# Mamba with attention on one core: engines issuing in program order, and a norm factor left in PSUM

## The chip, the cores and the metric

The kernel runs on one core of a Trainium2 chip. The metric is device time in microseconds (us), of one launch. The core has a tensor engine (TensorE, PE in the profile), a vector engine (VectorE, DVE), a scalar engine (ScalarE, ACT), GpSimd (POOL) and a queue for transfers (SyncE, SP). Each engine works through its own stream of instructions, and semaphores hold an instruction back until what it needs is there. TensorE writes its results to PSUM; the other data lies in SBUF.

The kernel is written with a layer that takes instructions in the order of the source and puts them into an order of its own for each engine, by a model of when each will be ready. Which instruction stands before which is thus decided when the program is built, not while it runs.

## The reference

A stack of four Mamba layers on 8 images of 256 channels and 32 x 32 positions, then a squeeze-and-excitation gate with batch normalization, then three attention layers. Only the Mamba part is touched:

```python
def _mamba(xs, lw, lb, iw, cw, cb, xw, dw, db, alog, dp, ow):
    mu = xs.mean(-1, keepdims=True)
    var = ((xs - mu) ** 2).mean(-1, keepdims=True)
    xn = (xs - mu) * jax.lax.rsqrt(var + 1e-05) * lw + lb
    xin, z = jnp.split(xn @ iw.T, 2, axis=-1)
    xc = ...                     # causal convolution over 4 positions, for each channel
    xin = jax.nn.silu(jnp.swapaxes(xc, 1, 2))
    proj = xin @ xw.T
    dt = jax.nn.softplus(proj[..., :DTR] @ dw.T + db)
    Bm = proj[..., DTR:DTR + DS]
    Cm = proj[..., DTR + DS:]
    A = -jnp.exp(alog)
    def step(h, t):
        dt_t, b_t, c_t, x_t = t
        h = h * jnp.exp(dt_t[..., None] * A) + (dt_t * x_t)[..., None] * b_t[:, None, :]
        return (h, jnp.einsum('bdn,bn->bd', h, c_t))
    ...                          # scan over the 1024 positions
    y = jnp.swapaxes(ys, 0, 1) + xin * dp
    return y * jax.nn.silu(z) @ ow.T
```

## The kernel before

The work is cut into 64 units: 4 layers, 8 samples, and 2 chunks of 512 positions each. A unit has 16 steps (2 halves `q` of the channels, 8 groups `g` of two state elements each), 1024 steps in all. In each step TensorE forms the drive `bx` of the recurrence, VectorE runs four scans, GpSimd multiplies the states by C, and TensorE sums them into `y` two steps later. Beside the steps of unit n run, cut into pieces by `yield`, the front part of unit n+2 (`inward`), the middle part of unit n+1 (`onward`) and the end of unit n-1 (`outward`). `AT` says in which of the 16 steps (slots 0 to 15) a piece comes.

The tile pools that matter: `wk1` has one buffer for each tag, `wk2` two; `ps_b` has two PSUM buffers for `bx`, `ps_m` two for everything tagged `mm`; `dap` has eight buffers for the decays `da` (two steps); `h` and `ct` have three.

```python
LAG, AHEAD = 2, 2
AT = ((inward, 2, (0, 1, 2, 3, 5, 6, 8, 9, 11, 12, 13, 14)), (onward, 1, (1, 3, 5, 7, 8, 9, 10, 11, 12)),
      (outward, -1, (3, 4, 6, 7, 9, 10, 11, 12, 13)))
DIAGONALS = (4, 5, 6, 10, 11, 12, 13, 14)
for i in range(len(steps) + LAG):
    n, at = divmod(i, per_unit)
    if i < len(steps):
        ahead(i + AHEAD)                    # transfer of ct; four Exp on ScalarE: da
        bxs = [forced(*steps[i], k) for k in range(2)]      # TensorE: bx
        for k in range(2):
            state(i, k, bxs[k])             # VectorE: four scans
        product(i)                          # ScalarE: hc (first chunk); GpSimd: h * ct
    if i >= LAG:
        ...                                 # TensorE: y += h of step i - LAG; VectorE: gate at the end of a half
    ...                                     # the pieces that AT names for this slot
    if at in DIAGONALS and n + 1 < len(units):
        diagonal(units[n + 1])              # GpSimd: dg, one of eight
```

The front part, with the norm (cut):

```python
pmu = ps_m.tile([P, T], F32, name=f"pmu{u}", tag="mm")          # slot 0
for k in range(CT):
    nc.tensor.matmul(pmu, lhsT=mean_w, rhs=x[:, k, :], start=(k == 0), stop=(k == CT - 1))
xn = wk1.tile([P, CT, T], F32, name=f"xn{u}", tag="xn")
nc.vector.tensor_tensor(xn, x, pmu.unsqueeze(1).to_broadcast([P, CT, T]), ALU.subtract)     # L126
sq = wk1.tile([P, CT, T], F32, name=f"sq{u}", tag="sq")
nc.scalar.activation(sq, xn, AF.Square)
yield
pvar = ps_m.tile([P, T], F32, name=f"pvar{u}", tag="mm")        # slot 1
for k in range(CT):
    nc.tensor.matmul(pvar, lhsT=mean_w, rhs=sq[:, k, :], start=(k == 0), stop=(k == CT - 1))
rstd = sq[:, 0, :]
nc.scalar.activation(rstd, pvar, AF.Ln, bias=eps)
nc.scalar.activation(rstd, rstd, AF.Exp, scale=-0.5)
nc.vector.tensor_tensor(xn, xn, rstd.unsqueeze(1).to_broadcast([P, CT, T]), ALU.mult)       # L136
yield
...     # slots 2 to 14: pin (TensorE) and its copy xr or sz (ScalarE), convolution pc (TensorE) and its copy xin
for q in range(DT // 2):
    nc.scalar.activation(s["xin"][q], s["xin"][q], AF.Silu)     # L183
nc.scalar.activation(sz, sz, AF.Silu)                           # L184
exp_ln_table()                                                  # L108, a table preload
```

The middle part (cut). `one` and `dtx` share a tag with one buffer, as do `ln` and `sq`:

```python
for q in range(DT // 2):                                        # slots 3 and 5, 7 and 8
    dt = wk3.tile([P, 2, T], F32, name=f"dt{u}_{q}", tag="dt")
    e = wk1.tile([P, 2, T], F32, name=f"e{u}_{q}", tag="e")
    for r in range(2):
        pd = ps_m.tile([P, T], F32, name=f"pd{u}_{i}", tag="mm")
        nc.tensor.matmul(pd, ...)
        nc.scalar.activation(e[:, r, :], pd, AF.Abs, bias=col(V_DB + i))        # L224
        nc.scalar.activation(dt[:, r, :], pd, AF.Relu, bias=col(V_DB + i))      # L225
    nc.scalar.activation(e, e, AF.Exp, scale=-1.0)              # L226
    yield
    one = wk1.tile([P, 2, T], F32, name=f"one{u}_{q}", tag="dtx")
    nc.scalar.activation(one, e, AF.Identity, bias=1.0)         # L229
    ln = wk1.tile([P, 2, T], F32, name=f"ln{u}_{q}", tag="sq")
    nc.scalar.activation(ln, one, AF.Ln)                        # L231
    nc.vector.scalar_tensor_tensor(e, one, 1.0, e, ALU.subtract, ALU.subtract)  # L233
    nc.vector.tensor_tensor(dt, dt, e, ALU.subtract)            # L234
    nc.vector.tensor_tensor(dt, dt, ln, ALU.add)                # L235
    yield
for q in range(DT // 2):                                        # slots 9 and 10, 11 and 12
    dtx = wk1.tile([P, 2, T], F32, name=f"dtx{u}_{q}", tag="dtx")
    for i in range(2):
        nc.gpsimd.tensor_tensor(tokens(dtx[:, i, :]), halves(s["dt"][q][:, i, :]), halves(xin[q][:, i, :]), ALU.mult)   # L241
    yield
    ...     # TensorE: pt, the transposes of dtx; ScalarE: their copy dtxT
    yield
```

The end part, `outward`: the output projection `po` in two pieces of two matmuls for each half of the channels, and L278, which adds it to the residual.

## Time and profile before

| | |
|---|---|
| time, median of 3 | 10693.12 us (10679.93 to 10694.59) |
| span of the profiled execution | 10677.8 us |
| Mamba phase, from the first scan to the end of the last | 93.60 to 8004.30 us |
| attention phase after it | 2673.5 us |
| granted TensorE clock over the span | 0.961 |
| table loads on ScalarE | 519, 1283 ns each |

The lines of a profile name an engine, a line of the kernel (L385), the operation, what it writes and reads (`h<-da,bx`), shape and count. A group's numbers are the time that the engine was busy with it, the mean duration of one in ns, and the idle time before it with what ended that. A timeline's numbers are the start and the duration in us; a bracket at the end is the idle time just before and what ended it. Matmuls are pipelined and their ends are modelled, so a busy TensorE isn't TensorE at its peak.

### The profile page before, as it was taken

What the parts mean: (1) busy time and instruction counts of PE and PEld (TensorE: products, weight loads), DVE (VectorE), ACT (ScalarE), POOL (GpSimd) and SP (SyncE); (2) the same over time, 40 slices, a digit from 0 to 9 for tenths busy, and PEclk for the clock granted to TensorE, in tenths of its full rate; (3) what the DMA queues carried; (4) which work ended last, traced back from release to release, by engine and by line L of the source; (5) the groups of instructions that cost most, each with busy time, mean ns of one, the idle gap of its engine ahead of it and who ended that gap; (6) DMA issues with size and microseconds to landing.
All of it is one profiled execution on the core that took longest, in us unless ns stands there. A gap on an engine that the chain in (4) does not pass through costs nothing. (4 is left out here: it accounts for less than half of the span.)

```text
span 10677.8 us, 237971 instructions
## 1 busy us (share of the span) xinstructions
PE 9676.4 (91%) x104946; PEld 4868.8 (46%) x104946; DVE 7570.7 (71%) x6419; ACT 6108.2 (57%) x8477; POOL 6709.4 (63%) x2563
## 2 busy tenths in 40 slices
PE   7999998999999989999998988888888999999998
PEld 3444444444444444444444444444443433444433
DVE  4878877777878877877887777777785455544554
ACT  5666666666666766666666666666652233333333
POOL 5777776677777767777776766666671344344346
PEclk9999999999999999999999999999999999999999
DMA  1222222222222222222222222222221000000000
GB/s 64 81 86 86 89 81 81 81 86 84 88 83 82 87 82 86 87 83 84 84 85 83 89 86 86 86 88 88 89 100 40 5 9 9 7 6 1 5 5 9
DMA packets 212557, 704.91 MB, mean 66 GB/s; under 512 B 32640, under 2 KB 33728, under 8 KB 210880
## 3 DMA queue, kind: packets, MB, share of 16 engines
q1 hardware_dynamic: 211520, 689.61, 19.4%
q8 instruction: 830, 13.60, 0.5%
q14 instruction: 207, 1.70, 0.1%
HBM read 637.09 MB, written 52.43 MB: 65 GB/s over the span
## 5 line engine op out<-in xcount | busy, mean ns | idle before, releaser
L392 POOL TENSOR_TENSOR h<-h,ct 128x2048 f32<-128x2048 f32 x1024 | 4683.9, 4581 | 2007.1 <-ACT hc L391 921.9
L335 ACT ACTIVATE da<-dt,A 128x512 f32<-128x512 f32 x4096 | 2847.4, 718 | 2298.7 <-DVE h L385 2283.8
L385 DVE TENSOR_TENSOR_SCAN h<-da,hc,bx 128x512 f32<-128x512 f32 x2048 | 2456.9, 1258 | 692.7 <-PE bx L325 579.9
L385 DVE TENSOR_TENSOR_SCAN h<-da,bx 128x512 f32<-128x512 f32 x2048 | 2332.0, 1198 | 722.9 <-PE bx L325 658.9
L325 PE MATMUL bx<-dg,dtxT 64*64 64x128 f32 x65536 | 2316.7, 281 | 306.1 <-DVE h L385 293.9
L325 PEld LDWEIGHTS bx<-dg,dtxT 64*64 64x64 f32 x65536 | 1950.1, 137 | 1131.0 <-issue 933.4
L349 PE MATMUL y<-h,twin 64*64 64x512 f32 x16384 | 2048.5, 599 | 72.2 <-POOL h L392 72.2
L571 ACT ACTIVATE fp<-fs 128x1024 f32<-128x1024 f32 x768 | 765.4, 1022 | 1435.7 <-PE fs L566 1408.0
L142 PE MATMUL pin<-xn,win 128*128 128x512 f32 x2048 | 1015.9, 619 | 9.8 <-DVE xn L136 5.8
L349 PEld LDWEIGHTS y<-h,twin 64*64 64x64 f32 x16384 | 718.0, 135 | 668.9 <-issue 511.4
L166 PE MATMUL pc<-xr,cd 64*64 64x512 f32 x4096 | 654.1, 695 | 207.8 <-DVE xo L278 207.8
L566 PE MATMUL fs<-fq,fk 32*128 32x512 f32 (+1 forms) x3072 | 723.4, 649 | 56.2 <-ACT fp L652 39.3
L588 DVE TENSOR_TENSOR fz<-fz,fp 128x1024 f32<-128x1024 f32 x384 | 531.3, 1384 | 331.0 <-ACT fp L571 327.0
L588 POOL TENSOR_TENSOR fz<-fz,fp 128x1024 f32<-128x1024 f32 x192 | 477.6, 2487 | 416.2 <-ACT fp L571 412.4
L142 PEld LDWEIGHTS pin<-xn,win 128*128 128x128 f32 x2048 | 349.0, 190 | 676.0 <-issue 405.6
L274 PE MATMUL po<-sz,wo 128*128 128x512 f32 x1024 | 561.7, 676 | 52.3 <-ACT dt L225 52.3
L582 PE MATMUL fo<-fp,fv 128*32 128x512 f32 (+1 forms) x3072 | 597.2, 615 | 0.0
L241 POOL TENSOR_TENSOR dtx<-dt,xin 128x512 f32<-128x512 f32 x256 | 432.8, 1716 | 224.8 <-ACT ln L231 222.2
L256 POOL TENSOR_TENSOR dg<-twin,bt 128x512 f32<-128x512 f32 x512 | 539.0, 1064 | 50.8 <-PE bx L325 37.9
L166 PEld LDWEIGHTS pc<-xr,cd 64*64 64x64 f32 x4096 | 230.4, 154 | 597.2 <-issue 274.5
L235 DVE TENSOR_TENSOR dt<-dt,ln 128x1024 f32<-128x1024 f32 x128 | 470.4, 3675 | 14.4 <-ACT da L335 0.9
L566 PEld LDWEIGHTS fs<-fq,fk 32*128 32x128 f32 (+1 forms) x3072 | 196.1, 185 | 469.4 <-issue 270.2
(391 smaller groups left out, 9160.8 us busy)
## 6 DMA issues: line engine op xcount, KB each, us to landing
ct<-cdr SPq DMA_DIRECT2D x1024, 512.0 KB, 3.7
spill<-xo SPq DMA_DIRECT2D x72, 512.0 KB, 5.3
x<-spill SPq DMA_DIRECT2D x48, 512.0 KB, 4.9
xo<-spill SPq DMA_DIRECT2D x48, 512.0 KB, 3.5
x<-in_x SPq DMA_DIRECT2D x16, 512.0 KB, 5.0
xo<-in_x SPq DMA_DIRECT2D x16, 512.0 KB, 3.7
res<-in_x SPq DMA_DIRECT2D x16, 512.0 KB, 4.2
fx<-spill SPq DMA_DIRECT2D x16, 512.0 KB, 6.4
```

Source lines behind the costliest of these rows:

```text
L142: nc.tensor.matmul(ps, lhsT=w["in"][:, k, e * P:(e + 1) * P], rhs=xn[:, k, :], start=(k == 0), stop=(k == CT - 1))
L166: nc.tensor.matmul(pcs[r][e * H:(e + 1) * H, :], lhsT=w["cd"][r * H:(r + 1) * H, j * K + k, :], rhs=xr[r * H:(r + 1) * H, e, k:k + T], sta ...
L274: nc.tensor.matmul(po, lhsT=w["out"][:, i, m * P:(m + 1) * P], rhs=s["sz"][:, i, :], start=(i == 0), stop=(i == DT - 1))
L325: nc.tensor.matmul(bx[r * H:(r + 1) * H, t:t + H, :], lhsT=s["dtxT"][q][h * H:(h + 1) * H, i, k, r * H:(r + 1) * H], rhs=s["dg"][g][h * H: ...
L335: nc.scalar.activation(da, s["dt"][q][:, i, :], AF.Exp, scale=s["w"]["A"][:, nn:nn + 1])
L349: nc.tensor.matmul(s["y"][r][i * H:(i + 1) * H, :], lhsT=twin[r * H:(r + 1) * H, :], rhs=h[r * H:(r + 1) * H, i, j, :], start=False, stop= ...
L385: nc.vector.tensor_tensor_scan(hs[i][:, k, j, :], das[i][2 * k + j], bx[:, :, j], init, ALU.mult, ALU.add)
L392: nc.gpsimd.tensor_tensor(h, h, cts.pop(i).unsqueeze(1).to_broadcast([P, 2, NG, T]), ALU.mult)
L566: nc.tensor.matmul(scs[h // 2][:, h % 2, :], lhsT=k[r:r + D, m, kt * P:(kt + 1) * P], rhs=q[r:r + D, m, half * T:(half + 1) * T], start=Tr ...
L571: nc.scalar.activation(p, scs[j], AF.Exp, scale=scale)
L582: nc.tensor.matmul(acc["o"][r:r + D, :], lhsT=v[:, kt, m * P + r:m * P + r + D], rhs=ps[h // 2][:, h % 2, :], start=(kt == 0), stop=(kt == ...
L588: add(acc["z"][j], acc["z"][j] if kt > 1 else probs[i - 1][j], ps[j], ALU.add)
```

## The change

It has three parts. All compute engines in the Mamba phase get a wrapper that pins each instruction behind the one that the source has before it on the same engine; the queue for transfers keeps the layer's freedom. The factor of the norm, Ln and Exp of the variance, is written back into `pvar` in PSUM and read from there by VectorE, so that it doesn't occupy `sq`, which `ln` needs as well. And the second residual tile of the last layer's end part, `sx`, takes a buffer of `x` in a pool of two instead of the single one of `dtx`, which in a fixed order would still be held by an earlier user. What it is for: the layer's order rests on a model of the durations; the source order is the author's own plan, which keeps functions of one table together and puts nothing in front of what was meant to come first.

```diff
--- before.py
+++ after.py
@@ -37,8 +37,28 @@
 G_SEB2, G_BNW, G_BNB, G_BQ1, G_BK1, G_BO1, G_BQ2, G_BK2, G_BQ3, G_BK3, G_BO3, G_N = range(0, 24, 2)
 
 
+class InOrder:
+
+
+    def __init__(self, tc, engine):
+        self.tc, self.engine = tc, engine
+
+    def __getattr__(self, name):
+        def call(*args, **kwargs):
+            return self.tc.keep_in_program_order(getattr(self.engine, name)(*args, **kwargs))
+
+        return call
+
+
+class Engines:
+    def __init__(self, tc):
+        nc = tc.nc
+        self.tensor, self.vector, self.scalar, self.gpsimd = (InOrder(tc, e) for e in (nc.tensor, nc.vector, nc.scalar, nc.gpsimd))
+        self.sync = nc.sync
+
+
 def mamba_phase(tc, ctx, a, spill, ident, gvec, stats):
-    nc = tc.nc
+    nc = Engines(tc)
     cst = ctx.enter_context(tc.tile_pool(name="m_cst", bufs=1))
     wp = ctx.enter_context(tc.tile_pool(name="m_w", bufs=1))
     wk1 = ctx.enter_context(tc.tile_pool(name="m_wk1", bufs=1))
@@ -105,7 +125,7 @@
         nc.sync.dma_start(w["out"], a["m_out"][l])
 
     def exp_ln_table():
-        tc.keep_in_program_order(nc.scalar.preload_act_table_set("natural_log_exp_and_others"))
+        nc.scalar.preload_act_table_set("natural_log_exp_and_others")
 
     def tokens(t):
 
@@ -130,10 +150,9 @@
         pvar = ps_m.tile([P, T], F32, name=f"pvar{u}", tag="mm")
         for k in range(CT):
             nc.tensor.matmul(pvar, lhsT=mean_w, rhs=sq[:, k, :], start=(k == 0), stop=(k == CT - 1))
-        rstd = sq[:, 0, :]
-        nc.scalar.activation(rstd, pvar, AF.Ln, bias=eps)
-        nc.scalar.activation(rstd, rstd, AF.Exp, scale=-0.5)
-        nc.vector.tensor_tensor(xn, xn, rstd.unsqueeze(1).to_broadcast([P, CT, T]), ALU.mult)
+        nc.scalar.activation(pvar, pvar, AF.Ln, bias=eps)
+        nc.scalar.activation(pvar, pvar, AF.Exp, scale=-0.5)
+        nc.vector.tensor_tensor(xn, xn, pvar.unsqueeze(1).to_broadcast([P, CT, T]), ALU.mult)
         yield
 
         def in_proj(e):
@@ -304,7 +323,7 @@
         exp_ln_table()
         yield
         for h in range(NCH):
-            y = x if h == c else wk1.tile([P, CT, T], F32, name=f"sx{b}_{h}", tag="dtx")
+            y = x if h == c else wk2.tile([P, CT, T], F32, name=f"sx{b}_{h}", tag="x")
             if h != c:
                 nc.sync.dma_start(y, spill[b][h])
             r = wk1.tile([P, CT, T], F32, name=f"res{b}_{h}", tag="e")
```

## The prediction

> **What bounds the kernel now.** I read the page's first part for the engines, then the table of stretches for where the time lies, then the groups of instructions, then the timeline of one unit, because in a loop of waits the averages say little.

> The page's busy times (engine, us, share of the span, instructions):

> ```profile
> PE 9676.4 (91%) x104946; PEld 4868.8 (46%) x104946; DVE 7570.7 (71%) x6419; ACT 6108.2 (57%) x8477; POOL 6709.4 (63%) x2563
> ```

> TensorE looks full, but its ends are modelled, so I count issue times instead. From the timeline, a pair of bx tiles takes 1.7 us to issue, a y set 1.72 (16 instructions of 512 columns, four at a time), one 128x512 matmul instruction 0.43. One unit (16 steps) then needs 16 x 3.43 for bx and y, 13.7 for pin, 6.9 each for pc and po, 3.4 each for pmu with pvar, pp and pd, 1.7 each for dd and pt: about 96 us. The table of stretches has the Mamba phase with its scans at 93.60 to 8004.30, 7910.7 us for 64 units, so 123 us a unit; the middle units, by the starts of their first scans, take 119 to 122. A fifth of TensorE's time is therefore waiting, and order can move it either way. VectorE is busy 93.5 us in the unit from 2561.86 to 2680.91, so it isn't the bound alone either: a step takes whatever is last in it.

> VectorE's timeline of that unit (start us, us, engine, line, ...); a step begins with its first scan (L385):

> ```profile
> 2568.02 4.55 DVE L385 TENSOR_TENSOR_SCAN h<-da,bx 128x512 f32<-128x512 f32 x4
> 2572.49 1.26 DVE L355 TENSOR_TENSOR sz<-y,sz 128x512 f32<-128x512 f32 x2
> 2574.70 4.46 DVE L136 TENSOR_TENSOR xn<-xn,sq 128x1024 f32<-128x1024 f32 x1 [0.94 <-ACT sq L135]
> ...
> 2596.14 2.33 DVE L385 TENSOR_TENSOR_SCAN h<-da,bx 128x512 f32<-128x512 f32 x2 [8.08 <-PE bx L325]
> 2598.39 1.20 DVE L233 SCALAR_TENSOR_TENSOR e<-one,e 128x1024 f32<-128x1024 f32 x1
> 2599.51 2.32 DVE L385 TENSOR_TENSOR_SCAN h<-da,bx 128x512 f32<-128x512 f32 x2
> 2601.75 1.20 DVE L234 TENSOR_TENSOR dt<-dt,e 128x1024 f32<-128x1024 f32 x1
> 2603.05 5.34 DVE L235 TENSOR_TENSOR dt<-dt,ln 128x1024 f32<-128x1024 f32 x1
> 2608.32 0.68 DVE L278 TENSOR_TENSOR xo<-po,xo 128x512 f32<-128x512 f32 x1
> 2608.92 4.54 DVE L385 TENSOR_TENSOR_SCAN h<-da,bx 128x512 f32<-128x512 f32 x4
> ```

> GpSimd's in the same unit:

> ```profile
> 2573.55 4.53 POOL L392 TENSOR_TENSOR h<-h,ct 128x2048 f32<-128x2048 f32 x1 [1.50 <-ACT hc L391]
> ...
> 2602.81 4.51 POOL L392 TENSOR_TENSOR h<-h,ct 128x2048 f32<-128x2048 f32 x1 [6.05 <-ACT hc L391]
> ```

> Two things are to be seen. L136 and the last L235, which take 1.2 us when free, end 1.1 us after GpSimd's product ends (2578.08 and 2607.32): they were locked out until then. And the scheduler has put L233 between two scans, a step earlier than the source has it, because it also moved L229 and L231 forward on ScalarE. ScalarE's timeline there:

> ```profile
> 2593.00 1.07 ACT L226 ACTIVATE e<-e 128x1024 f32<-128x1024 f32 x1
> 2594.16 1.06 ACT L229 ACTIVATE one<-e 128x1024 f32<-128x1024 f32 x1
> 2595.25 1.06 ACT L231 ACTIVATE ln<-one 128x1024 f32<-128x1024 f32 x1
> ```

> The groups that the change removes or shortens:

> ```profile
> L136 DVE TENSOR_TENSOR xn<-xn,sq 128x1024 f32<-128x1024 f32 x64 | 283.7, 4432 | 76.5 <-ACT sq L135 76.5
> ...
> L126 DVE TENSOR_TENSOR xn<-x,pmu 128x1024 f32<-128x1024 f32 x64 | 77.9, 1217 | 56.3 <-PE pmu L124 56.3
> ```

> ```profile
> L335 ACT ACT_TABLE_LOAD x186 | 238.6, 1283 | 3.3
> L183 ACT ACT_TABLE_LOAD x126 | 161.7, 1283 | 2.2
> L231 ACT ACT_TABLE_LOAD x62 | 79.5, 1283 | 1.1
> ```

> [...] L136 (two SBUF inputs) 4432 ns, L126 (same shape, one input in PSUM) 1217 ns. [...] the trace has 1283 ns, and the next activation starts at once, so I use 1.28. [...]

> **The change, part by part.** I work a unit by hand, step by step (slots 0 to 15), from the two issue orders and the durations above. Fixed offsets from the trace, from a step's first scan: scans end at 4.6; TensorE's y runs 0.5 to 2.4; the four da activations follow the scans and end at 5.3; GpSimd's product runs 5.0 to 9.6 (5.5 to 10.1 on a sample's first chunk, after hc); the next first scan comes 1.3 after the next bx starts. Slot lengths before are mean values of 35 middle units, sum 120.4.

> - *Table loads.* Program order keeps all Silu together: 372 of 519 loads go, 372 x 1.283 = 477 us of ScalarE. None of it ends a step, since ScalarE idles 2283.8 us behind the scans anyway: worth about 0. Its price: Silu, loads and all, sit at the end of slot 14 (6.6 us), which delays sq and so pvar in slot 1 by some 0.8.
> - *Norm factor in PSUM.* L136 falls to 1.2, 64 x 3.2 = 206 us of VectorE. Slot 1 becomes bound by TensorE (pvar, then pp until 7.8, then bx: 9.0, with the late sq 9.8 instead of 11.4), but TensorE has lost its lead and slot 2 takes 6.3 instead of 4.7. Together 16.1 against 16.1: 0.
> - *Slot 3.* po no longer fits bx matmuls into its waits for ScalarE: 11.7, against 12.3 (some of those had a lower clock): 0 to -0.6.
> - *Slots 4 and 5.* The softplus tail leaves slot 4 (12.9 to 5.7) and comes back in slot 5. There ScalarE must first do the da, then the two xin (pc ends at 5.9), then one and ln: one is ready at 8.4. VectorE stands from 4.6. By then the product holds the lock until 9.6 or 10.1; then L233, L234, L235 (3.75) and one dg of 1.05 in between: 14.6 to 15.0 instead of 6.3. Sum of the pair +1.3.
> - *Slot 6.* TensorE is ahead: 4.7 instead of 7.4, -2.7.
> - *Slot 7.* The second pd needs the PSUM buffer of the first, which ScalarE frees at 6.6; the second half of po now waits behind it instead of filling the gap: pd to 7.7, po to 9.6, bx, scan: 10.8 instead of 9.2, +1.6.
> - *Slot 8.* VectorE waits for one (7.1), then for the product (9.6 or 10.1), then 3.75: 13.5 to 14.0 instead of 9.4, +4.4.
> - *Slots 10 and 12.* GpSimd now does dtx (2 x 1.7) only after the product of the step: it ends some 7.0 into slot 10 and 7.5 into slot 12, and TensorE's pt stands in front of bx. 9.1 instead of 5.2, and 9.4 instead of 8.0: +5.3.
> - *Others* (0, 9, 11, 13, 14, 15): within 0.3 of before.

> Sum: 0 - 0.3 + 1.3 - 2.7 + 1.6 + 4.4 + 5.3 = +9.6 us a unit. Over some 60 ordinary units +575. At the start, unit 0 and unit 1 are no longer overlapped with the first steps (first scan at 93.6 now): about +20. Layer changes and the pooling steps of the last layer wait for transfers in both: 0, with room for either sign. The attention phase (2673.5 us) is not touched. 10693 + 595 = 11288; hand work of this sort finds waits more easily than the slack that swallows them, so I take 11240.

> **Rivals.** (1) The savings count: 477 us of ScalarE and 206 of VectorE are real, and if they shortened steps, the time would be near 10200 to 10450. Against it: VectorE's greatest wait in the loop is for bx on TensorE (1238.8 us), and ScalarE's is for VectorE's scans. (2) The order hardly matters: the two streams differ in few places, and what is lost in slots 8 and 10 is made good by TensorE running ahead in slots 9 and 11, as it does in slot 6; then 10600 to 10850. Against it: bx has two buffers, so TensorE can be ahead by one step at most. (3) Worse than I have it: ps_m has two buffers, and a stall on one engine shifts the phase against GpSimd's lock, so that VectorE is blocked more than once in a step; then 11500 and more.

> **Range and chances.** The slot sums carry about 3 us a unit, some 190 us, and the start and layer changes 50: 10950 to 11480. Faster by over 2% needs rival 1, 0.05; within 2% rival 2, 0.1; slower 0.85.

> **What would show it.** VectorE: L233 behind a whole set of four scans with a wait for ScalarE's one of 2 to 5 us before it and a length of 2 to 4 us, locked out; L136's successor at 1.2 us. ScalarE: about 147 table loads. TensorE: pt waiting for GpSimd's dtx, pd for ScalarE. Unit starts about 130 us apart. Steps of 120 us or less would prove the sum wrong; a dtx that ends before the y of its step, or a softplus tail of under 4 us after the scans in slot 8, would name the failed term.

## The result, and the profile after

The changed kernel takes 11493.38 us (median of 4 runs, 11486.32 to 11512.26), the kernel before 10686.53 us (median of its 4 runs, 10650.78 to 10694.59): 1.0765 times, 95% interval 1.0737 to 1.0793. The direction is the predicted one; the time lies 253 us above the predicted 11240 and 13 us above the range.

First the page's line of busy times (engine, us, share of the span, instructions), which answers to the first line shown of before:

```profile
PE 9909.1 (86%) x104946; PEld 4932.9 (43%) x104946; DVE 7397.4 (64%) x6419; ACT 5691.6 (50%) x8105; POOL 6625.5 (58%) x2563
```

VectorE and ScalarE do less work than before (by 173 and 417 us), so the loss is waiting. TensorE has the same 104946 instructions and 233 us more busy time: the same work ran slower. Both halves of the story are in this line.

The groups that the change was to shorten, and those that it made longer (busy us, mean ns of one | idle us before, and what ended it):

```profile
L48 DVE SCALAR_TENSOR_TENSOR e<-one,e 128x1024 f32<-128x1024 f32 x128 | 424.9, 3319 | 409.4 <-ACT one L48 409.4
...
L48 ACT ACT_TABLE_LOAD x147 | 188.6, 1283 | 5.3 <-PE pvar L48 2.1 <-PEq L1043 0.7
L48 PE MATMUL pt<-ident,dtx 128*128 128x128 f32 x1024 | 177.7, 300 | 275.7 <-POOL dtx L48 214.2 <-ACT sz L48 60.2
...
L48 DVE TENSOR_TENSOR xn<-xn,pvar 128x1024 f32<-128x1024 f32 x64 | 78.2, 1221 | 105.7 <-ACT pvar L48 105.7
```

Every instruction now has line 48, the wrapper's, so one goes by the names of the tiles. Both promised savings are there: 519 - 147 = 372 table loads are gone, and the norm's multiplication takes 78.2 us instead of 283.7. Against them, `e` (L233 before) went from 1233 to 3319 ns and has 409.4 us of waiting for `one` in front of it, and `pt` waits 214.2 us for GpSimd's `dtx`.

VectorE in the unit from 2857.60 to 2993.70 (start, us), steps 5 and 8:

```profile
2899.26 4.55 DVE L48 TENSOR_TENSOR_SCAN h<-da,bx 128x512 f32<-128x512 f32 x4 [0.47 <-PE bx L48]
2907.40 3.03 DVE L48 SCALAR_TENSOR_TENSOR e<-one,e 128x1024 f32<-128x1024 f32 x1 [3.58 <-ACT one L48]
2910.46 2.10 DVE L48 TENSOR_TENSOR dt<-dt,e 128x1024 f32<-128x1024 f32 x1
2912.66 1.23 DVE L48 TENSOR_TENSOR dt<-dt,ln 128x1024 f32<-128x1024 f32 x1
...
2932.46 4.55 DVE L48 TENSOR_TENSOR_SCAN h<-da,bx 128x512 f32<-128x512 f32 x4 [0.48 <-PE bx L48]
2939.43 4.15 DVE L48 SCALAR_TENSOR_TENSOR e<-one,e 128x1024 f32<-128x1024 f32 x1 [2.41 <-ACT one L48]
```

and ScalarE and GpSimd in step 5:

```profile
2905.15 1.27 ACT L48 ACTIVATE xin<-pc,vec 128x512 f32<-128x512 f32 x2 [0.50 <-PE pc L48]
2906.31 1.06 ACT L48 ACTIVATE one<-e 128x1024 f32<-128x1024 f32 x1
2907.40 1.06 ACT L48 ACTIVATE ln<-one 128x1024 f32<-128x1024 f32 x1
```

```profile
2904.79 4.56 POOL L48 TENSOR_TENSOR h<-h,ct 128x2048 f32<-128x2048 f32 x1 [0.23 <-ACT hc L48]
```

The scans end at 2903.81, `one` at 2907.37; then `e`, free 1.23 us, takes 3.03 and ends 1.1 us after the product does (2909.35). The lockout is the one that L136 had before (4432 ns; with its factor in PSUM 1221).

The mean step lengths of the same 35 middle units, from first scan to next first scan, beside the prediction's ("others" taken as before):

| step | 1+2 | 3 | 4 | 5 | 6 | 7 | 8 | 10 | 12 | others | unit |
|---|---|---|---|---|---|---|---|---|---|---|---|
| before | 16.1 | 12.3 | 12.9 | 6.3 | 7.4 | 9.2 | 9.4 | 5.2 | 8.0 | 33.7 | 120.4 |
| predicted | 16.1 | 11.7 | 5.7 | 14.8 | 4.7 | 10.8 | 13.8 | 9.1 | 9.4 | 33.7 | 129.8 |
| after | 17.3 | 14.3 | 5.7 | 14.2 | 4.6 | 13.8 | 13.4 | 9.2 | 8.7 | 33.9 | 135.1 |

The 812.5 us between the two spans (11490.3 - 10677.8) split into 39 before the first scan (93.60 to 132.55), 774 in the Mamba phase (7910.7 to 8685.05), and under 1 anywhere else.

Steps 3 and 7, where the prediction is 2.6 and 3.0 us short, are TensorE's. First step 3 of that unit, then its po of step 6 with step 7 behind it:

```profile
2883.40 0.41 PE L48 MATMUL pb<-ident,proj 16*128 16x16 f32 x4
2885.14 1.22 PE L48 MATMUL pd<-proj,wdt 16*128 16x512 f32 x4 [1.32 <-ACT xr L48]
2887.61 3.78 PE L48 MATMUL po<-sz,wo 128*128 128x512 f32 x4 [1.26 <-ACT dt L48]
2891.32 2.56 PE L48 MATMUL bx<-dg,dtxT 64*64 64x128 f32 x44
```

```profile
2910.33 1.88 PE L48 MATMUL po<-sz,wo 128*128 128x512 f32 x4
2916.28 1.10 PE L48 MATMUL bx<-dg,dtxT 64*64 64x128 f32 x32 [4.06 <-DVE h L48]
...
2920.23 3.67 PE L48 MATMUL y<-h,twin 64*64 64x512 f32 x16
2923.83 1.39 PE L48 MATMUL pd<-proj,wdt 16*128 16x512 f32 x2
2926.58 1.12 PE L48 MATMUL pd<-proj,wdt 16*128 16x512 f32 x2 [1.36 <-ACT dt L48]
2927.63 3.62 PE L48 MATMUL po<-sz,wo 128*128 128x512 f32 x4
```

The same four po instructions take 1.88 us at 2910.33 and 3.78 and 3.62 us behind the waits; a y set takes 3.67 instead of 1.9. The table of stretches for these two steps (stretch, us, PE busy, granted clock, DMA):

```profile
2879.10:2893.47 14.37, 11.79 (x100) 0.77 0.21 74
2918.27:2932.46 14.19, 12.61 (x104) 0.66 0.23 74
```

The clock has two values in the trace's records, 1.0 and 0.5, in stretches of 3.4 us or a multiple of it. Counted over the Mamba phase there are 700 us of half clock before and 1659 after (1652 in the expectations below, which leave out a stretch that began just before the first scan); in the middle units, 6.4 us in a step 3 and 8.8 in a step 7 on average (2.6 and 0.55 before).

### The profile page after: what moved, and what is told of

It reads as the page before. It is cut to its first block, busy times and chain, and to the rows that moved or that the text cites. A ratio compares the mean times of both kernels' runs of the same rounds, so it can differ in the third digit from the quotient of the medians.

```text
span 11490.3 us, 237784 instructions
## 1 busy us (share of the span) xinstructions
PE 9909.1 (86%) x104946; PEld 4932.9 (43%) x104946; DVE 7397.4 (64%) x6419; ACT 5691.6 (50%) x8105; POOL 6625.5 (58%) x2563
## 4 chain that ended last, share of the span: by engine, by line
PE 54%; DVE 25%; ACT 9%; POOL 6%; issue 5%; DMA 1%; SPq 0%; DVEq 0%; POOLq 0%; ACTq 0%
DVE h L48 17%; PE bx L48 10%; PE y L48 8%; PE po L48 5%; PE fs L585 5%; POOL h L48 4%; DVE e L48 4%; PE fo L601 4%; PE pin L48 3%; ACT da L48 2%; PE fo L689 2%; PE fs L665 2%; PE pc L48 2%; PE pp L48 2%; DVE dt L48 2%
## 5 line engine op out<-in xcount | busy, mean ns | idle before, releaser
L48 ACT ACTIVATE da<-dt,A 128x512 f32<-128x512 f32 x4096 | 2911.3, 722 | 3309.1 <-DVE h L48 3303.9
L48 PE MATMUL bx<-dg,dtxT 64*64 64x128 f32 x65536 | 2382.2, 298 | 710.1 <-DVE h L48 703.7
L48 PEld LDWEIGHTS bx<-dg,dtxT 64*64 64x64 f32 x65536 | 2072.6, 149 | 1549.3 <-issue 1436.1
L48 PEld LDWEIGHTS y<-h,twin 64*64 64x64 f32 x16384 | 636.8, 142 | 800.7 <-issue 697.0
L585 PE MATMUL fs<-fq,fk 32*128 32x512 f32 (+1 forms) x3072 | 722.2, 648 | 56.3 <-ACT fp L671 39.3
L48 PE MATMUL po<-sz,wo 128*128 128x512 f32 x1024 | 695.9, 817 | 75.3 <-ACT dt L48 75.3
L48 DVE SCALAR_TENSOR_TENSOR e<-one,e 128x1024 f32<-128x1024 f32 x128 | 424.9, 3319 | 409.4 <-ACT one L48 409.4
L48 PE MATMUL pc<-xr,cd 64*64 64x512 f32 x4096 | 466.6, 589 | 0.0
L48 PEld LDWEIGHTS po<-sz,wo 128*128 128x128 f32 x1024 | 228.4, 241 | 452.5 <-issue 321.9
L48 PE MATMUL pt<-ident,dtx 128*128 128x128 f32 x1024 | 177.7, 300 | 275.7 <-POOL dtx L48 214.2
```

The lines of the kernel that those rows point to most:

```text
L48: return self.tc.keep_in_program_order(getattr(self.engine, name)(*args, **kwargs))
L585: nc.tensor.matmul(scs[h // 2][:, h % 2, :], lhsT=k[r:r + D, m, kt * P:(kt + 1) * P], rhs=q[r:r + D, m, half * T:(half + 1) * T], start=Tr ...
```

## The experiments

Three theories. **A**: the written order makes stalls (the tail behind the scans, po behind pd, dtx behind the product, da ahead of what is due), and TensorE's clock halves behind them. **B**: `pvar` with the norm's factor keeps one of two PSUM buffers busy, and that is what costs. **C**: the clock falls with load, not with idleness. Diffs are against the changed kernel unless said otherwise; "before" of each comparison was run again on the same chip.

**psum_only and order_only: the two parts alone.**

```diff
 # psum_only: the kernel before, with
-        rstd = sq[:, 0, :]
-        nc.scalar.activation(rstd, pvar, AF.Ln, bias=eps)
+        nc.scalar.activation(pvar, pvar, AF.Ln, bias=eps)
 ...
 # order_only: the changed kernel with these lines as before
```

> The kernel before with one part of the change: the norm's factor stays in PSUM, the scheduler keeps its freedom. Theory A (the order of issue makes the loss, by stalls and the half clock of TensorE that follows them): VectorE's multiplication falls from 4.4 to 1.2 us, slot 1 gets about 2 us shorter and slot 2 nearly as much longer; 10650, between 0.99 and 1.0 of before. Theory B (the held PSUM buffer makes the loss, since the pool has two): 11200 or more, with matmuls waiting for the multiplication.

> The changed kernel with the norm's factor back in SBUF: program order alone. Theory A: the multiplication is again locked out by GpSimd and takes 4.4 us, slot 1 longer and slot 2 shorter; 11500 to 11600, so the whole loss is here. Theory B: near 10750.

Measured: psum_only 10738.17 us, 1.0053 (1.0036 to 1.0070); order_only 11400.02 us, 1.0674 (1.0653 to 1.0695). B falls as the main cause: nearly the whole loss is the order. But both numbers expected under A were missed (10650, and 11500 to 11600), because the PSUM part isn't free: 0.5% alone and about 0.9% on top of the order. In psum_only steps 1 and 2 together stay as they were (16.05 to 15.95 us), as the prediction had it, but step 3 grows by 0.9, and has 5.2 us of half clock instead of 2.6. That TensorE's lost lead brings this about wasn't tried. Nor was the third part of the change, `sx`, tried alone; it stands in order_only too.

**act_in_order: only ScalarE pinned**, the other three engines left to the scheduler.

> The changed kernel with ScalarE alone held to program order. Theory A: the table loads fall to about 147, but the softplus tail is late on ScalarE and VectorE must wait for it, while GpSimd and TensorE keep their better orders: 10850 to 11200. If table loads were on the path: under 10400. If ScalarE's order did not matter: 10650 to 10750.

Measured: 10898.18 us in one run, before 10681.54, so 2.0% more: a quarter of the loss, of which psum_only has 0.5% already. The loads are 147 here too, and the kernel is slower all the same. The rest of the loss needs the other engines' order too.

**filler: the same order and waits, but TensorE kept busy in them.** Matmuls with weights of zero, added to a y that is being summed, stand in TensorE's waits of steps 3, 6 and 7. They add zero and only take time.

```diff
+        nc.tensor.matmul(y[0][0:H, :], lhsT=zero[0:H, :], rhs=s["xin"][q][0:H, 0, :], start=False, stop=False)
 # one behind pb, one behind the first pd (step 7) or the second (step 3), four at the end of step 6
```

> The changed kernel with matmuls of zero weights put into TensorE's waits (one after pb, one after the first pair of pd, one between the second pair, four at the end of slot 6); they add zero to y. Theory A with the half clock as a consequence of idleness: less time at half clock than the 1652 us of the changed kernel's Mamba phase, slot 3 near 12 instead of 14.3 and slot 7 near 11 instead of 13.8, in all 11150 to 11350. Rival C (the clock falls by load or power, whatever TensorE did before): half clock as long or longer, 11500 or more.

Measured: 11377.61 us, 1.0653 (1.0632 to 1.0674): 890 instructions more, and some 116 us less. Half clock in the Mamba phase falls from 1659 to 1201 us, in steps 3 and 7 from 6.4 and 8.8 to 4.0 and 4.0; the steps fall from 14.3 and 13.8 to 13.4 and 12.75 us. Steps 3 and 7 of one unit, and step 3 of the next, in the same columns as above:

```profile
2822.30:2835.43 13.13, 12.67 (x111) 0.87 0.21 81
2859.97:2872.44 12.47, 10.76 (x106) 0.86 0.16 48
2959.74:2974.51 14.77, 14.30 (x112) 0.77 0.20 72
```

More matmuls and a higher clock speak against C, though what load weights of zero make was not measured. The kernel `best` below leaves C no room: the same 104946 instructions in a shorter time, at a higher clock (0.976 over the span, 0.921 after the change), and the table in the last section has half clock behind the emptiest stretches. But the fillers don't always work (in the last line the clock is as low as after the change; so it is in step 3 of 6 of the 35 middle units), much of the half-clock time stays, and they take time themselves: the gain is less than expected.

**po_moved: po out of the waits.** Whole in step 4, and ahead of pd in step 7.

```diff
-                if i == 1:
+                if i == 1 and m:
                     yield
...
-          (outward, -1, (3, 4, 6, 7, 9, 10, 11, 12, 13)))
+          (outward, -1, (4, 6, 7, 9, 10, 11, 12, 13)))
...
-        for what, d, when in AT:
+        for what, d, when in (AT if at != 7 else AT[::-1]):
```

> The changed kernel with po alone moved: whole in step 4 instead of split over steps 3 and 4, and ahead of pd in step 7 instead of behind it. In the changed kernel TensorE's clock record shows half speed for 6.4 of the 14.3 us of step 3 and 8.8 of the 13.8 us of step 7. If po's place makes those waits and the half clock after them, step 3 falls below 10.5 and step 7 below 11.5, step 4 grows to some 8: at least 3.5 us a unit, 225 us or more, so 11,150 to 11,300. If po's place is not the cause, the two steps stay above 13.

Measured: 11012.57 us, 1.0303 (1.0270 to 1.0337), more than expected: step 3 from 14.3 to 9.0, step 7 from 13.8 to 10.2, step 4 from 5.7 to 8.0, a unit from 135.1 to 127.0. Half clock in step 3 falls from 6.4 to 1.2 us, in step 7 from 8.8 to 4.7. The group of po, then steps 3 and 7 of one unit:

```profile
L48 PE MATMUL po<-sz,wo 128*128 128x512 f32 x1024 | 487.1, 608 | 0.0
```

```profile
2711.30:2719.76 8.46, 7.13 (x103) 1.00 0.17 62
2746.14:2756.12 9.98, 9.87 (x103) 0.79 0.16 54
```

After the change po took 695.9 us, 817 ns each (676 before it); it is now at 608 with the same matmuls. What half clock is left in step 7 follows the stall that the tail makes in steps 5 and 6 (the 4.06 us wait above), which this kernel still has. Later runs bear that out: tail_early takes this stall away and leaves po, and has 4.6 us of half clock in step 7; all_three moves both, and has none.

**hc15: step 15's da behind the copy of the last states.**

```diff
-            ahead(i + AHEAD)
+            if at != 15:
+                ahead(i + AHEAD)
 ...
             product(i)
+            if at == 15:
+                ahead(i + AHEAD)
```

> The changed kernel with one thing moved: the four da that ScalarE issues in step 15 stand behind that step's copy of the last states instead of in front of it, so that the copy waits for the Silu block alone. If that queue is what makes step 1 of a sample's second chunk 13.5 us instead of the first chunk's 8.9, it falls to 9 to 11 there and a unit by 1 to 2 us on average: 60 to 130 us less than the changed kernel, 11,360 to 11,430. If it is not, step 1 keeps its 13.5.

ScalarE at the end of a first chunk, in the changed kernel and then in hc15:

```profile
2994.81 1.28 ACT L48 ACT_TABLE_LOAD   x1
2996.10 2.56 ACT L48 ACTIVATE da<-dt,A 128x512 f32<-128x512 f32 x4
2998.57 0.18 ACT L48 COPY hc<-h 128x4 f32<-128x4 f32 x1
```

```profile
2937.05 1.28 ACT L48 ACT_TABLE_LOAD   x1
2938.34 0.20 ACT L48 COPY hc<-h 128x4 f32<-128x4 f32 x1
2938.45 1.94 ACT L48 ACTIVATE da<-dt,A 128x512 f32<-128x512 f32 x3
```

The copy is what GpSimd's product waits for, and the y of step 1 waits for that product. In the changed kernel:

```profile
2998.88 13.50 POOL L48 TENSOR_TENSOR h<-h,ct 128x2048 f32<-128x2048 f32 x3 [4.11 <-ACT hc L48]
```

```profile
3003.48 3.34 PE L48 MATMUL y<-h,twin 64*64 64x512 f32 x16 [2.91 <-POOL h L48]
```

Measured: 11352.41 us, 1.0621 (1.0587 to 1.0656), 8 us better than the expected range. Step 1 of second chunks falls from 12.9 (the expectation has 13.5) to 9.7 us, first chunks keep their 8.9, and a unit loses 2.0 us.

**dtx_first: dtx before GpSimd's product in steps 9 and 11.**

```diff
+            if at in (9, 11) and onward in side:
+                next(side[onward], None)
             product(i)
 ...                                  # the piece is left out of its old place behind the product
```

> The changed kernel with one thing moved: the pieces that hold dtx stand before GpSimd's product in steps 9 and 11. If the product in front of dtx is what makes step 10 9.2 us and step 12 8.7, step 10 falls to 5.2 to 5.6 and step 12 to about 8.0, while step 9 keeps its 5.8 because TensorE comes into it ahead: 4 us a unit, about 250 us, so 11,200 to 11,280. If the wait only changes its place, as it did between steps 9 and 10 of tail_early, it gives under 100 us.

Measured: 11258.41 us, 1.0552 (1.0521 to 1.0582). The sum is as expected, its parts are not: step 10 falls from 9.2 to 6.7 only, step 12 from 8.7 to 8.0, which is 3.2 us of the 4.5 that a unit loses. Steps 3, 7, 11 and 13 are shorter too, and step 8 is 0.9 longer.

**tail_early and tail_dtx: the softplus tail between the scans**, then dtx as well.

```diff
             nc.scalar.activation(e, e, AF.Exp, scale=-1.0)
-            yield
             one = wk1.tile(...)          # and ln: in steps 3 and 7
-            nc.vector.scalar_tensor_tensor(e, one, 1.0, e, ALU.subtract, ALU.subtract)
-            ...
+            tails.append(tail)           # the same three operations
 ...
                 state(i, k, bxs[k])
+                if k == 0 and tails:
+                    tails.pop()()
```

> The changed kernel, strictly in order, with the softplus tail moved by hand: one and ln are written directly behind the exponential (steps 3 and 7), and VectorE's three tail operations stand between the first two and the last two scans of steps 4 and 8, where the scheduler had put the first of them. Theory A (stalls that the order makes): steps 5 and 8 fall from 14.2 and 13.4 us to about 7 and 10, some 10 us a unit of which 2 or 3 come back in step 4; about 11,000 us. Theory C (load and power): the time stays above 11,350.

> tail_early, and the pieces with dtx stand before GpSimd's product in steps 9 and 11. Theory A: steps 10 and 12 fall from 9.2 and 8.7 to about 5.2 and 8, and the late product costs nothing: 5 us a unit, 300 us less than tail_early, so about 10,700 (10,550 to 10,850). If the pair of steps 9 and 10 only shifts the wait to the product, it stays within 100 us of tail_early.

Measured, one run each: 11137.7 and 11031.5 us beside 10697.38. A applies, but gave less than expected, and the second expectation missed. Steps 5 and 8 fell as expected or further, to 7.5 and 8.3 us, step 4 took back 3.2, and a unit fell by 6.1. Step 9 went from 5.8 to 9.2, and TensorE shows why:

```profile
2804.96 1.95 PE L48 MATMUL bx<-dg,dtxT 64*64 64x128 f32 x32 [3.05 <-DVE h L48]
2806.62 2.84 PE L48 MATMUL y<-h,twin 64*64 64x512 f32 x16
2809.26 3.64 PE L48 MATMUL pc<-xr,cd 64*64 64x512 f32 x32
```

In the changed kernel the long step 8 had let TensorE start step 9 ahead, so pc was hidden: there it ended before the first scan of step 9, at 2946.08.

```profile
2940.24 3.62 PE L48 MATMUL pc<-xr,cd 64*64 64x512 f32 x32
```

With step 8 short, pc ends step 9, and dtx has time to finish behind it. That is why dtx, worth 4.5 us a unit by itself, was worth 1.9 here.

**all_three and all_four: po as well, then da behind the pieces.** all_four also puts `ahead(i + AHEAD)` behind a step's pieces, except in step 14.

> tail_dtx, and po is issued whole in step 4 and before pd in step 7 (nothing of it in step 3). Theory A: step 3 falls from 14.3 to about 11 because po no longer stands in front of bx there, step 7 from 13.8 to about 11: 300 to 500 us less than tail_dtx, about 10,250 (10,050 to 10,450), and the time in which the records show half the TensorE clock falls from 1650 us to under 700. If half the clock is not due to TensorE's idleness, it stays above 1200.

> all_three, and ScalarE's four da of the step after next are issued behind the step's pieces, except in step 14. Theory A: ScalarE's pieces no longer wait for the scans, 1 to 2 us a unit less: 60 to 130 us under all_three. If VectorE then waits for da instead, it is slower than all_three.

Measured: all_three 10419.08 us, 0.9754 (0.9694 to 0.9813); all_four 10108.58 us, 0.9463 (0.9405 to 0.9521). Half clock: 758 us (under 700 expected) and 498. all_three fell by 612, not 300 to 500; all_four by 310 more, not 60 to 130, mostly in second chunks (units from 121.6 to 113.1 us), whose step 1 fell from 13.7 to 9.6. VectorE in step 8 of all_four, with the whole tail between the scans, where the scheduler had put only its first operation:

```profile
2480.22 2.33 DVE L48 TENSOR_TENSOR_SCAN h<-da,bx 128x512 f32<-128x512 f32 x2 [2.37 <-PE bx L48]
2482.63 1.23 DVE L48 SCALAR_TENSOR_TENSOR e<-one,e 128x1024 f32<-128x1024 f32 x1
2483.89 1.23 DVE L48 TENSOR_TENSOR dt<-dt,e 128x1024 f32<-128x1024 f32 x1
2485.22 1.23 DVE L48 TENSOR_TENSOR dt<-dt,ln 128x1024 f32<-128x1024 f32 x1
```

Three operations of 1.23 us and no lockout.

**free_four: all_four's source with the scheduler back.**

> all_four's source, with the compiler's scheduler deciding the order of the four engines again, as before the change. If what the change lost was the place of the work in the written order and not strictness as such, all_four's written order is as good as the scheduler's or better: free_four takes 10,050 to 10,350 us. If strictness itself costs (no engine may go around a wait), the scheduler gains on it once more, by some 5%: 9,600 to 9,750.

Measured: 10220.09 us, 0.9578 (0.9551 to 0.9606), against all_four's 0.9463. That is as expected: strictness as such costs nothing here, and with a good written order it is 1.1% better than the scheduler's order of the same source. In free_four step 4 alone is 13.2 us (9.6 in all_four).

**best and best_sb.** From all_four:

```diff
-                if i == 1 and m:
-                    yield
...
-          (outward, -1, (4, 6, 7, 9, 10, 11, 12, 13)))
+          (outward, -1, (4, 8, 9, 10, 11, 12, 13)))       # second half of po whole in step 8
...
-            nc.scalar.copy(s["st"]["h"][:, q, g, :, :], h[:, :, :, T - 1])
+            nc.gpsimd.tensor_copy(s["st"]["h"][:, q, g, :, :], h[:, :, :, T - 1])
```

> all_four, and two things more: the second half of po is issued whole in step 8, where TensorE waits for VectorE's softplus tail, instead of in steps 6 and 7, and the copy of the last states is done by GpSimd, ahead of its own product, instead of ScalarE. Steps 6, 7 and 8 from 7.3, 7.6 and 8.4 to about 5.6, 6.0 and 9.3, step 12 from 7.2 to 6.7: 2 to 2.5 us a unit, about 130 us less than all_four: 9,960 (9,880 to 10,080).

> best, with the norm's factor back in SBUF as before the change. Step 1 grows by 1.5 to 3 us where GpSimd's lock holds the multiplication up, step 2 shrinks by 1.7 as TensorE gets its lead back. If the sum of the two is what counts, it is within 0.5% of best; if the hand-made order has no slack left, 1% slower.

Measured: best 9965.13 us, 0.9326 (0.9302 to 0.9350); best_sb 9960.74 us, 0.9318 (0.9295 to 0.9341). The two can't be told apart: in this written order the place of the norm's factor doesn't matter (step 1 is 1.5 us longer and step 2 1.5 shorter), while in the first one it made 0.9%. The page's line of best:

```profile
PE 9208.3 (93%) x104946; PEld 4656.2 (47%) x104946; DVE 7126.9 (72%) x6419; ACT 5376.2 (54%) x7593; POOL 6653.9 (67%) x3075
```

TensorE does its 104946 instructions in 9208.3 us, against 9909.1 after the change; 328 us of half clock are left. Step 7 fell to 4.7 us, but step 8 grew to 11.5 where 9.3 was expected. VectorE there, and GpSimd:

```profile
2423.88 2.79 DVE L48 SCALAR_TENSOR_TENSOR e<-one,e 128x1024 f32<-128x1024 f32 x1 [0.99 <-ACT one L48]
```

```profile
2421.03 4.54 POOL L48 TENSOR_TENSOR h<-h,ct 128x2048 f32<-128x2048 f32 x1
```

Step 7 is so short that its product starts only after the first scan of step 8 (2420.55), is still running when `e` comes, and locks it out (2.79 instead of 1.23 us). Steps 6 to 8 together gained 1.6 us a unit, step 9 another 1.0 and step 3 0.5; the whole unit went from 112.8 to 110.0.

## Why the prediction was right and wrong

The mechanism was right: stalls that the written order makes, in the steps that were named (in step 5 VectorE stands 3.58 us before `e`, which waits for `one`; in step 7 TensorE stands 1.36 us before the second pd, with po and bx behind it). Three terms of the sum were too small, those of steps 3, 7 and 1; the first two because every matmul was reckoned at full clock.

- **Table loads, norm factor.** Right: 372 loads and 206 us of VectorE went, and neither shows as a gain: act_in_order has the loads of the changed kernel and is slower than before, and psum_only lengthens step 2 by about as much as it shortens step 1. Rival 1, that the savings count, falls by both.
- **Steps 4, 5, 6 and 8** (the tail leaves 4, comes back late in 5 and 8, locked out by the product). Right, and within 0.6 us each: predicted 5.7, 14.8, 4.7 and 13.8; measured 5.7, 14.2, 4.6 and 13.4. tail_early undoes it and steps 5 and 8 fall to 7.5 and 8.3.
- **Steps 10 and 12** (dtx behind the product). Right: 9.2 and 8.7 against 9.1 and 9.4; dtx_first gives back 3.2 us in these two and 4.5 in the unit. Rival 2, that steps 9 and 11 make the loss good, falls: they keep their length (5.8 and 5.8 before, 5.8 and 5.9 after).
- **Step 3: "11.7, against 12.3 (some of those had a lower clock)"** is the first term that was mis-sized. It saw the lower clock in the kernel before and then reckoned after at full clock. Measured 14.3. In the unit shown, po costs 3.78 us instead of 1.88 and the bx behind it some 0.8 more (the scan follows their start by 2.15 us, 2891.32 to 2893.47, where the prediction has 1.3): 2.7 us, which is the gap (14.37 - 11.7).
- **Step 7: "pd to 7.7, po to 9.6, bx, scan: 10.8"** is the second. The wait of the second pd and po behind it are as described; y at 3.67 instead of 1.9 and po at 3.62 instead of 1.88 are 3.5 us, and the gap is 3.4 (14.19 - 10.8). po_moved and filler show both terms: without po behind the waits, or with work in them, clock and steps recover, with filler in part.
- **Step 1: "with the late sq 9.8"** is the third. Silu does sit at the end of step 14, but what it delays most isn't sq. The copy of the last states stands behind it and four da in ScalarE's queue, GpSimd's product waits 4.1 us for the copy, and y, ahead of pvar on TensorE, waits for the product. First chunks have 8.9 us, second chunks 12.9; hc15 takes it away (step 1 and 2 together then 15.7, predicted 16.1).
- **The sum.** +9.6 a unit were predicted for the middle units, +14.7 measured: 2.6 + 3.0 + 1.2 from these three, the other terms -1.4 together, the rest by rounding (the table's sum is +9.4). The 35 middle units give 5.1 x 35 = 179 us too little, the start 19 (+39, predicted +20), the other units some 20. The deduction from 11288 to 11240, for slack that swallows waits, was in the wrong direction: a stall here brought on a second loss, the half clock (1659 us against 700 before).
- **Rival 3** ("11500 and more") has nearly the measured number, but not its reason: the extra time lies in TensorE's clock and ScalarE's queue, not in VectorE being locked out more often. Steps 5 and 8 came out shorter than predicted, and the operations that were seen locked out before or after the change, the norm's multiplication and the softplus tail, took less in all: 868.0 us of VectorE after the change, 1086.2 before.

## What to carry to other kernels

A strict order is only as good as the place of every instruction in it: the same pinning gives 1.0765 or 0.9326, by where some twenty lines stand and one small copy on another engine. When you work out a stall on TensorE by hand, add the half clock that the trace shows behind it to the wait (here 6.4 us in a step 3 and 8.8 in a step 7), and look at what is then issued there; put short, independent work into waits (filler gained 116 us) and the long matmuls out of them (po_moved gained 481). Matmuls of 16 rows didn't do as such work here: pb and pd ran in 46% of the 3.41 us ahead of the slow po in step 3, and the clock fell. And look for the small instruction that others wait for (here a copy of 0.18 us) standing behind large ones in a queue.

## What the hardware showed that was not expected

The prediction reckoned every matmul at full clock; the records show half clock in stretches of 3.4 us and multiples. No long wait stands ahead of the slow po in step 3: there are two of 1.32 and 1.26 us, with pb and pd of 16 rows between them, and then a half-clock stretch from 2886.9 to 2893.7. In this trace a sparse window was enough.

| cell at | share of the cell | cells | next cell at half clock |
|---|---|---|---|
| full clock | under 30% | 2024 | 2024 |
| full clock | 30 to 55% | 2470 | 1135 |
| full clock | 55% or more | 28294 | 2 |
| half clock | under 75% | 1079 | 1079 |
| half clock | 75 to 90% | 919 | 377 |
| half clock | 90% or more | 2734 | 108 |

In before and after alone, the six rows are 291 of 291, 176 of 313, 0 of 3563, 140 of 140, 67 of 189 and 15 of 361.

Both slow po come out of this. The cell ahead of the one in step 3, 2883.45 to 2886.87, has matmuls in 46% of it, all of them pb and pd; that ahead of the one in step 7, 2924.41 to 2927.83, in 60%, but the others than pd in only 6%. If pb and pd are counted like the others, full-clock cells of up to 90% (in before) and of up to 99% (in all_four) are followed by half clock: counted so, the share no longer tells the cells apart. Half clock went with a stall's place in the grid as well. In filler, step 3 has 3.4 us of half clock in the 29 middle units in which it begins 1.6 to 2.6 us into a cell, and 6.8 us in the 6 in which it begins 2.8 to 3.2 us into one: in that run the fillers helped less in the late cells.
